# A graph attention kernel: queries stored once in DRAM, and stacked queries and keys loaded by two DMAs of 64 partitions each

## The chip, the cores and the metric

The kernel runs on one core of one Trainium2 chip. The metric is the device time of one execution in microseconds (us), lower is better. The core has five engines with instruction streams of their own: TensorE (PE in the profile, with PEld for its weight loads), VectorE (DVE), ScalarE (ACT), GpSimd (POOL) and SyncE (SP, which here only issues DMAs). The transfers of SP, ACT and POOL are carried by the same 16 DMA engines.

## What is computed

Two layers work on 16 graphs of 1024 nodes with 256 features, in float32.

```python
# layer 0: masked attention with 8 heads of 32 features
h = relu(layernorm(x))
Q, K, V = h @ Wq.T + bq, h @ Wk.T + bk, h @ Wv.T + bv
scores = Q @ K.T * 32 ** -0.5                  # per graph and head, 1024 x 1024
attn = softmax(where(adj == 0, -inf, scores))
x = x + (attn @ V) @ Wo.T + bo
# layer 1: attention whose scores depend on the kind of edge
h = relu(layernorm(x))
e_k = leaky_relu((h * a_k) @ h.T, 0.2)         # k = 0..3
alpha = softmax(e_{adj-1} where adj in 1..4, else -9e15)
x = x + alpha @ h
```

`adj` holds 0 and 1 here, so layer 1 needs only `e_0`. The kernel checks that at run time and has a general path, which the profiled execution does not take.

## The kernel before, in words

A **tile** is 128 nodes (rows) of one graph. There are 8 tiles in a graph and 128 in all, and the main loop `for s in range(B * NT + 1)` does the attention of one tile per pass. Inside a pass, a loop over the 8 heads writes out by hand (`tc.manual_schedule()`) what each engine does, in order. Besides the attention of tile `s` (`now`) a pass holds the rest of the tile before (`was`), layer 1 of the tile that is nine behind (`edge`), and the preparation of a tile of the next graph (`piece`, `piece_was`: normalise, transpose, project to Q, K and V).

**Scores with split numbers.** TensorE multiplies in the format float32r. To keep precision, Q and K are each held as two halves, a rounded number and the remainder. A head has 32 features, so the two halves of Q times the two halves of K are 4 x 32 = 128 rows of contraction, just the 128 partitions: `Attend.scores` (L455) multiplies `qt[:, h, :]` (128 partitions by 128 queries) with `keysets[b][h]` (128 partitions by 1024 keys), in two matmuls of 512 columns. In `qt` each feature's two halves must stand twice, and so must they in the keys, so that every half of Q meets every half of K.

**How the stacks are made.** The projections give features on partitions. The halves are written to DRAM and read back in the stacked order:

- Keys: `write_keys` (L325) writes both halves to `kds[b]`, laid out `[NC, P, 2, N]`. `load_key` (L355) reads the 64 rows of a head (32 features by 2 halves), each twice, by one DMA of 128 partitions, 512 KB, on SP's queue.
- Queries: `write_queries` (L319) writes the halves to `qds[b]` *twice*, by two DMAs (one per block of 128 features) of 256 KB on POOL's queue, into `[NT, NC, P, 2, 2, P]`. For the first graph `split` does the same on the queues of SP and ACT (L292), four 512 KB DMAs on each. `load_queries` (L422) then reads a tile's stack, 128 partitions by 8 heads by 512 bytes, by one DMA on SP's queue.

**When the stacks are loaded.** `qt` has two buffers; the next tile's is loaded in the middle of a pass (at head 3), half a pass before its use. A head's keys have a single buffer (`k0` to `k7`) that holds a whole graph's keys for 8 passes, so the keys of the next graph can be loaded only as the last pass of a graph (`t == NT - 1`) is done with them. `KEY_STEPS = (6, 9, 10, 13, 16, 20, 22, 24)` sets the places in half-heads: keys 0 to 3 in the last pass of a graph, keys 4 to 7 in the first pass of the next. This turn from graph to graph comes 15 times. Key `h` is first used at head `h` of the first pass.

**SP's queue** is served in order. In each pass it also carries 20 DMAs `pT<-blocks` (`placed`, L381): after VectorE has transposed 32x32 blocks of a tile's probabilities, four DMAs each take 32 partitions of `blocks`, 128 KB, and lay them out over 128 partitions of `pT`. Four of a pass's eight heads and the layer 1 tile go this way; the other heads are transposed on TensorE (L574). SP also writes `x1d` (L536) and `out` (L691).

Of the kernel before, what the change touches and what calls it, by code (L numbers as in the profile page):

```python
# [8 lines left out]
F32 = mybir.dt.float32  # L9
# [8 lines left out]
P = 128  # L18
HEADS = 8
HD = 32  # L20
# [22 lines left out]
def gnn_kernel(  # L43
# [18 lines left out]
    nc = tc.nc  # L62
    B, N, D = x.shape
    NT = N // P
    NC = D // P
# [15 lines left out]
    dram = ctx.enter_context(tc.tile_pool(name="dram", bufs=2, space=bass.MemoryType.DRAM))  # L81
# [64 lines left out]
    def norm_of(mv):  # L146

        g = nc.gpsimd
        n = mv.shape[1]

        def place(name, dtype=F32):
            if n <= 4:
                return small.tile([P, 4], dtype, tag=name, name=name)[:, :n]
            places.append(name)
            return many[:, len(places) * n - n : len(places) * n].bitcast(dtype)

        places = []
        if n > 4:
            many = work.tile([P, D], F32, tag="wide", name="many", bufs=1)

        ve = place("ve")
        g.tensor_scalar(ve, mv[:, :, 1], EPS, None, ALU.add)
        r = place("r")
        g.tensor_tensor(r, ve, less_half.to_broadcast([P, n]), ALU.pow)
        shift = place("shift")
        g.tensor_tensor(shift, mv[:, :, 0], r, ALU.mult)
        g.tensor_scalar(shift, shift, -1.0, None, ALU.mult)
        return r, shift
# [12 lines left out]
    qds, kds, vs, keysets, weights = {}, {}, {}, {}, {}  # L181

    class Piece:
# [66 lines left out]
        def project(self, which, oc):  # L250
            wT, bias = ((weights["wkT"], bk_t), (weights["wqT"], bq_t))[which]
            b, w = self.b, self.n * P
            if b not in kds:
                kds[b] = dram.tile([NC, P, 2, N], F32, tag="kd", name=f"kd_{b}")
            if b not in qds and which == 1:
                qds[b] = dram.tile([NT, NC, P, 2, 2, P], F32, tag="qd", name=f"qd_{b}")
            if self.n > 1:
                ps = ps_tr.tile([P, w], F32, tag="tr", name="proj")
            else:
                ps = (late, early)[which][:, oc * P : (oc + 1) * P]  # L260
            for fc in range(NC):
                nc.tensor.matmul(
                    ps,
                    lhsT=wT[:, fc, oc * P : (oc + 1) * P],
                    rhs=(self.hT, self.hTm)[which][:, fc, :],
                    start=(fc == 0),
                    stop=(fc == NC - 1),
                )

            self.projected.append((which, oc, ps, bias))  # L270
# [10 lines left out]
        def split(self):  # L281
            which, oc, ps, bias, halves, parts = self.halved.pop(0)
            nc.vector.scalar_tensor_tensor(
                parts[:, 1], ps, bias[:, oc : oc + 1], parts[:, 0].bitcast(F32), ALU.add, ALU.subtract
            )
            halves = halves.bitcast(F32)
            if which == 0:
                self.write_keys(oc, halves, nc.sync)
            elif self.n > 1:
                to = qds[self.b][self.first : self.first + self.n, oc]  # L290
                for twice in range(2):
                    (nc.sync, nc.scalar)[twice].dma_start(  # L292
                        out=to[:, :, twice].rearrange("t p w n -> p t (w n)"),
                        in_=halves.rearrange("p (t x) -> p t x", t=self.n),
                    )
            else:
                self.queries.append((oc, halves))

# [7 lines left out]
        def halve(self, which):  # L306
            halves = self.buffer(3, [P, NC, 2, P], F32R)
            nc.gpsimd.tensor_copy(halves[:, :, 0], self.full)
            nc.gpsimd.tensor_tensor(halves[:, :, 1], self.full, halves[:, :, 0].bitcast(F32), ALU.subtract)  # L309
            places = [(oc, halves[:, oc].bitcast(F32).rearrange("p w n -> p (w n)")) for oc in range(NC)]  # L310
            if which == 0:
                for oc, place in places:
                    self.write_keys(oc, place, nc.gpsimd)
            else:
                self.queries = places

        def write_queries(self):
            for oc, halves in self.queries:
                nc.gpsimd.dma_start(  # L319
                    out=qds[self.b][self.first, oc].rearrange("p u w n -> p u (w n)"),  # L320
                    in_=halves.unsqueeze(1).to_broadcast([P, 2, 2 * P]),
                )

        def write_keys(self, oc, halves, queue):
            queue.dma_start(  # L325
# [26 lines left out]
    def load_key(b, h):  # L352
        kt = keys.tile([P, N], F32R, tag=f"k{h}", name=f"k{h}_{b}")
        c, r = divmod(h, GROUP)
        nc.sync.dma_start(  # L355
            out=kt.bitcast(F32),
            in_=kds[b][c, r * HD : (r + 1) * HD]
            .rearrange("d w n -> (d w) n").unsqueeze(1).to_broadcast([2 * HD, 2, N]),
        )
        keysets.setdefault(b, {})[h] = kt  # L360


# [47 lines left out]
    class Attend:  # L410
# [7 lines left out]

        def load_queries(self):
            self.qt = work.tile([P, HEADS, P], F32R, tag="qt")  # L420
            q = qds[self.b][self.t].rearrange("c (r d) u w n -> (d u w) (c r) n", d=HD)
            nc.sync.dma_start(out=self.qt.bitcast(F32), in_=q)  # L422

        def load(self):
            self.adj = work.tile([P, N], I32, tag="adj", bufs=1)
# [344 lines left out]
    with tc.manual_schedule():  # L770
# [14 lines left out]
        r, shift = norm_of(mv)  # L785
# [8 lines left out]
        for which in range(2):  # L794
            for piece in first:
                for oc in range(NC):
                    piece.project(which, oc)
                    piece.high()
                    piece.split()
            if which == 0:  # L800
                for h in range(HEADS):
                    load_key(0, h)
# [16 lines left out]
        for s in range(B * NT + 1):  # L819
            b, t = divmod(s, NT)  # L820

            def load_keys(h, end):
                if t == NT - 1 and b + 1 < B and 2 * h + end in KEY_STEPS:
                    load_key(b + 1, KEY_STEPS.index(2 * h + end))
                if t == 0 and 0 < b < B and 2 * (HEADS + h) + end in KEY_STEPS:
                    load_key(b, KEY_STEPS.index(2 * (HEADS + h) + end))
# [216 lines left out]
```

## Time and profile before

| | |
|---|---|
| median of 3 runs | 3138.88 us (3132.21 to 3140.22) |
| the profiled execution | 3143.69 us, of which the span from its first to its last instruction is 3141.9 us |
| PE busy | 2941.3 us, 94% of the span, mean granted clock 0.984 |
| ACT, DVE, POOL busy | 2598.8, 2512.8, 2172.4 us |
| DMA traffic | 729.22 MB, mean 232 GB/s |
| `pT<-blocks` (SP) | 2560 DMAs of 128 KB, 3.6 us from issue to landing |
| `k<-kd` (SP) | 128 DMAs of 512 KB, 6.1 us |
| `qt<-qd` (SP) | 128 DMAs of 512 KB, 4.4 us |
| `qd<-halves` (POOL) | 240 DMAs of 256 KB, 3.0 us |

A row of the profile names the line of the kernel, the engine, the operation and the tiles (`out<-in`). In a timeline the columns are start, duration, engine, line, operation, count, and in brackets the idle time before and what ended it. A row of windows gives a stretch of the span, its length, each engine's busy time in it (with its number of instructions), the granted clock of TensorE as a share, the mean busy share of the 16 DMA engines, and the GB/s that they moved. The DMA share adds up packets by their starts, so in a short stretch it can pass 1.

### The profile page before, as it was taken

Reading aid. Unit: us, or ns where it says so; the run is one execution under the profiler, and the core shown is the slowest. Engines: PE = TensorE matmul, PEld = TensorE weight load, DVE = VectorE, ACT = ScalarE, POOL = GpSimd, SP = SyncE. Lnnn points to the kernel's source line nnn. Section 1 sums busy time; section 2 is a strip of 40 time slices with the busy share of each in tenths; the row PEclk is TensorE's granted clock in tenths of the full one; section 3 lists DMA queues with packets and bytes.
Section 4 is the critical chain, followed back from the end, with each engine's and each line's share of the span. In section 5 each row is a group of like instructions: output and inputs, shape, how many; then the busy total and the mean of one; then the engine's idle time right before and its main releaser. Section 6 shows DMA issues by size and latency. Waiting matters only on the chain. (4 is left out here: it accounts for less than half of the span.)

```text
span 3141.9 us, 95789 instructions
## 1 busy us (share of the span) xinstructions
PE 2941.3 (94%) x36210; PEld 2202.9 (70%) x36210; DVE 2512.8 (80%) x4391; ACT 2598.8 (83%) x5157; POOL 2172.4 (69%) x2995
## 2 busy tenths in 40 slices
PE   5888999899999999999999999999999999998987
PEld 3666777677676777777777676777767777676663
DVE  4777888788787887878888787888878788787874
ACT  3888989889888988889889898888978888787871
POOL 2666777777777776777777777777767777675542
PEclk8999999999999999999999999999999999999999
DMA  6676787877878787787877878787787877777663
GB/s 214 208 245 212 230 272 220 270 217 230 255 229 263 223 263 225 226 268 223 270 227 235 251 234 257 228 258 229 234 261 215 271 223 227 245 232 239 185 174 96
DMA packets 634692, 729.22 MB, mean 232 GB/s; under 512 B 67376, under 2 KB 565424, under 8 KB 634224
## 3 DMA queue, kind: packets, MB, share of 16 engines
q1 hardware_dynamic: 565152, 510.86, 54.5%
q0 software_dynamic: 66960, 210.04, 20.5%
q8 instruction: 291, 4.77, 0.6%
q10 hardware_dynamic: 2112, 2.10, 0.2%
q14 instruction: 177, 1.45, 0.1%
HBM read 252.98 MB, written 134.22 MB: 123 GB/s over the span
## 5 line engine op out<-in xcount | busy, mean ns | idle before, releaser
L467 DVE CUSTOM_DVE_ANT_0 p<-s,neg 128x1024 f32<-128x1024 f32 x1024 | 1235.6, 1207 | 274.5 <-PE s L455 241.3
L475 ACT ACTIVATE p<-p,nmx 128x1024 f32<-128x1024 f32 x1024 | 1182.2, 1155 | 205.0 <-DVE nmx L467 202.5
L455 PE MATMUL s<-k,qt 128*128 128x512 f32 x2048 | 764.9, 455 | 107.9 <-DMA k<-kd 72.5
L376 DVE STREAM_TRANSPOSE blocks<-p 128x1024 f32<-128x1024 f32 x520 | 643.7, 1238 | 20.5 <-ACT p L663 10.6
L575 ACT COPY pT<-trp 128x512 f32<-128x512 f32 x1024 | 547.0, 590 | 106.2 <-PE trp L574 106.2
L510 PE MATMUL acc<-pT,v 128*32 128x128 f32 x16384 | 559.0, 281 | 37.1 <-DMA pT<-blocks 22.1
L510 PEld LDWEIGHTS acc<-pT,v 128*32 128x32 f32 x16384 | 472.6, 113 | 156.5 <-issue 82.9
L574 PE MATMUL trp<-ident,p 128*128 128x128 f32 x4096 | 531.2, 273 | 1.6 <-ACT pT L575 1.5
L574 PEld LDWEIGHTS trp<-ident,p 128*128 128x128 f32 x4096 | 478.1, 140 | 73.2 <-ACT pT L575 3.1
L435 POOL TENSOR_SCALAR neg<-adj 128x1024 bf16<-128x1024 int32 x128 | 467.6, 3653 | 79.5 <-ACT neg L447 70.2
L681 PE MATMUL acc<-h,pT 128*32 128x256 f32 x8192 | 494.7, 383 | 8.8 <-DVE ot L690 8.8
L455 PEld LDWEIGHTS s<-k,qt 128*128 128x128 f32 x2048 | 324.3, 192 | 215.5 <-issue 79.5
L681 PEld LDWEIGHTS acc<-h,pT 128*32 128x32 f32 x8192 | 241.8, 110 | 211.9 <-issue 63.8
L659 POOL TENSOR_TENSOR sel<-sel,less 128x1024 f32<-128x1024 f32 x120 | 286.6, 2388 | 64.9 <-ACT less L648 44.9
L616 PE MATMUL s<-h1T,ha 128*128 128x512 f32 (+2 forms) x744 | 272.8, 490 | 2.6 <-ACT h1T L553 1.3
L657 POOL TENSOR_SCALAR less<-top 128x1 f32<-128x1 f32 x120 | 31.6, 264 | 274.5 <-DVE top L639 274.5
L319 POOL DMA_DIRECT2D qd<-halves x240 | 177.0, 777 | 58.7 <-POOL halves L309 31.8
L494 POOL COPY wide<-rec 128x256 f32<-128x256 f32 x128 | 53.9, 421 | 226.5 <-DVE rec L492 226.5
L475 ACT ACTIVATION_READ_ACCUMULATOR p<-p,nmx 128x1 f32 x1024 | 202.7, 198 | 0.0
L325 POOL DMA_DIRECT2D kd<-halves x240 | 171.7, 764 | 35.4 <-POOL halves L309 35.4
L309 POOL TENSOR_TENSOR halves<-full,halves 128x256 fp32r<-128x256 f32 x240 | 176.3, 735 | 20.6
L648 ACT ACTIVATE less<-sel 128x1024 f32<-128x1024 f32 x120 | 127.0, 1058 | 65.6 <-DVE top L639 65.6
(120 smaller groups left out, 4238.8 us busy)
## 6 DMA issues: line engine op xcount, KB each, us to landing
pT<-blocks SPq DMA_DIRECT2D x2560, 128.0 KB, 3.6
k<-kd SPq DMA_DIRECT2D x128, 512.0 KB, 6.1
qt<-qd SPq DMA_DIRECT2D x128, 512.0 KB, 4.4
adj<-in_adj POOLq DMA_DIRECT2D x127, 512.0 KB, 5.1
qd<-halves POOLq DMA_DIRECT2D x240, 256.0 KB, 3.0
kd<-halves POOLq DMA_DIRECT2D x240, 128.0 KB, 4.0
xb<-in_x POOLq DMA_DIRECT2D x128, 128.0 KB, 4.4
x1d<-x SPq DMA_DIRECT2D x128, 128.0 KB, 4.0
```

The lines of the kernel that those rows point to most:

```text
L319: nc.gpsimd.dma_start(out=qds[self.b][self.first, oc].rearrange("p u w n -> p u (w n)"), in_=halves.unsqueeze(1).to_broadcast([P, 2, 2 * P]),)
L376: nc.vector.transpose(blocks.rearrange("p b j q -> p j b q"), p)
L435: nc.gpsimd.tensor_scalar(self.neg, self.adj, 0.0, MASKED, ALU.is_equal, ALU.mult)
L455: nc.tensor.matmul(self.ps[:, cols], lhsT=self.qt[:, h, :], rhs=keysets[self.b][h][:, cols], start=True, stop=True,)
L467: nc.vector.tensor_tensor_reduce(out=p, in0=sides[h in (4, 6)], in1=self.neg, scale=-SCALE, scalar=FLOOR, op0=ALU.add, op1=ALU.min, accum_ ...
L475: nc.scalar.activation(p, p, AF.Exp, bias=nmx, scale=-1.0, accum_out=self.sums[:, h : h + 1])
L510: nc.tensor.matmul(sums_place[r * HD : (r + 1) * HD, g * P : (g + 1) * P], lhsT=vs[self.b][:, j, place_of(h) : place_of(h) + HD], rhs=self ...
L574: nc.tensor.transpose(tr[:, j, :], p[:, jj * P : (jj + 1) * P], ident)
L575: copy(pT[:, half * 4 : half * 4 + 4, :], tr)
L616: nc.tensor.matmul(self.side[:, cols], lhsT=self.ha[:, c, :], rhs=h1T[:, c, cols], start=(c == 0), stop=(c == NC - 1),)
L659: nc.gpsimd.tensor_tensor(self.sel, self.sel, self.less, ALU.subtract)
L681: nc.tensor.matmul(sums_place[a * HD : (a + 1) * HD, :], lhsT=self.pT[:, j, a], rhs=h1s[self.b][:, j, :], start=(j == 0), stop=(j == NT - 1),)
```

## The change

Queries are stored once: `qds[b]` loses the axis of copies, a tile's two blocks of 128 features go out by one POOL DMA instead of two (256 KB in all instead of 512 KB), and the first graph's queries are written by ACT's queue alone (SP's four DMAs go). The stacks are read by two DMAs of 64 partitions each. For `qt`, both DMAs read the same 64 rows (32 features by 2 halves), one to partitions 0 to 63 and one to 64 to 127. For the keys, the first takes the 32 rows of the rounded half, each twice, and the second the 32 rows of the remainder, each twice. The order of the 128 contraction rows changes in both operands alike.

```diff
@@ Piece.project
-                qds[b] = dram.tile([NT, NC, P, 2, 2, P], F32, tag="qd", name=f"qd_{b}")
+                qds[b] = dram.tile([NT, NC, P, 2 * P], F32, tag="qd", name=f"qd_{b}")
@@ Piece.split
                 to = qds[self.b][self.first : self.first + self.n, oc]
-                for twice in range(2):
-                    (nc.sync, nc.scalar)[twice].dma_start(
-                        out=to[:, :, twice].rearrange("t p w n -> p t (w n)"),
-                        in_=halves.rearrange("p (t x) -> p t x", t=self.n),
-                    )
+                nc.scalar.dma_start(
+                    out=to.rearrange("t p x -> p t x"), in_=halves.rearrange("p (t x) -> p t x", t=self.n)
+                )
@@ Piece.halve
-                self.queries = places
+                self.queries = halves.bitcast(F32).rearrange("p c w n -> p c (w n)")
@@ Piece.write_queries
-            for oc, halves in self.queries:
-                nc.gpsimd.dma_start(
-                    out=qds[self.b][self.first, oc].rearrange("p u w n -> p u (w n)"),
-                    in_=halves.unsqueeze(1).to_broadcast([P, 2, 2 * P]),
-                )
+            nc.gpsimd.dma_start(
+                out=qds[self.b][self.first].rearrange("c p x -> p c x"), in_=self.queries
+            )
@@ load_key
-        nc.sync.dma_start(
-            out=kt.bitcast(F32),
-            in_=kds[b][c, r * HD : (r + 1) * HD]
-            .rearrange("d w n -> (d w) n").unsqueeze(1).to_broadcast([2 * HD, 2, N]),
-        )
+        for w in range(2):
+            nc.sync.dma_start(
+                out=kt[w * 2 * HD : (w + 1) * 2 * HD].bitcast(F32),
+                in_=kds[b][c, r * HD : (r + 1) * HD, w].unsqueeze(1).to_broadcast([HD, 2, N]),
+            )
@@ Attend.load_queries
-            q = qds[self.b][self.t].rearrange("c (r d) u w n -> (d u w) (c r) n", d=HD)
-            nc.sync.dma_start(out=self.qt.bitcast(F32), in_=q)
+            q = qds[self.b][self.t].rearrange("c (r d) (u n) -> (d u) (c r) n", d=HD, u=2)
+            for w in range(2):
+                nc.sync.dma_start(out=self.qt[w * 2 * HD : (w + 1) * 2 * HD].bitcast(F32), in_=q)
```

## The prediction

> **What bounds the kernel now.** I read the page's engine line, then windows of single passes, the tensor engine's waits, and the timelines of PE and SP around one turn from graph to graph.
>
> ```profile
> PE 2941.3 (94%) x36210; PEld 2202.9 (70%) x36210; DVE 2512.8 (80%) x4391; ACT 2598.8 (83%) x5157; POOL 2172.4 (69%) x2995
> 1543.80:1571.30 27.50, 23.60 (x290) 18.17 (x286) 19.63 (x35) 20.04 (x40) 18.05 (x28) 0.94 0.94 311
> ...
> 1618.10:1640.80 22.70, 22.70 (x289) 17.31 (x285) 19.39 (x35) 20.65 (x42) 17.48 (x24) 1.00 0.75 228
> ```
>
> The last row is an ordinary pass (the fourth of a graph): 22.70 us, all of them PE's, with the DMA engines busy 0.75 of the time. The row above is the first pass of a graph: 27.50 us, PE 23.60, clock 0.94, DMA share 0.94. Summed over the 15 turns, the first passes take 441.30 us with PE busy 350.26, so 6.1 us idle each; the fourth passes take 340.80 us with 339.27. So ordinary passes are PE's alone; only the 15 turns, and the start, have time to win or lose to a DMA.
>
> ```profile
> PE s L455 <- DMA k<-kd: 72.5, 36, 5.8
> PE acc L510 <- DMA pT<-blocks: 22.1, 25, 2.2
> ...
> PE s L455 <- DMA qt<-qd: 15.5, 3, 14.7
> ```
>
> Those are PE's waits for DMAs (total, times, longest): keys first. Of the wait for `qt`, 14.7 us are one wait, at the start. One turn, PE and then SP:
>
> ```profile
> 1552.26 0.70 PE L455 MATMUL s<-k,qt 128*128 128x512 f32 x2 [1.30 <-DMA k<-kd]
> ...
> 1568.74 0.70 PE L455 MATMUL s<-k,qt 128*128 128x512 f32 x2 [1.21 <-DMA k<-kd]
> ```
>
> ```profile
> 1532.49 0.55 SPq L355 DMA_DIRECT2D k<-kd  x1
> 1533.87 2.54 SPq L381 DMA_DIRECT2D pT<-blocks  x4
> 1536.52 0.54 SPq L422 DMA_DIRECT2D qt<-qd  x1
> 1537.15 1.90 SPq L355 DMA_DIRECT2D k<-kd  x2
> ...
> 1545.67 0.93 SPq L355 DMA_DIRECT2D k<-kd  x1
> 1546.71 3.76 SPq L381 DMA_DIRECT2D pT<-blocks  x4
> ...
> 1562.65 0.54 SPq L422 DMA_DIRECT2D qt<-qd  x1
> 1563.24 0.72 SPq L355 DMA_DIRECT2D k<-kd  x1
> ```
>
> PE waits for key 3 (issued 1545.67, used 1552.26) and key 7 (1563.24, 1568.74). Both took 5.5 to 6.6 us to use, where a quiet 512 KB load (`qt<-qd`) lands in 4.4. What they wait in is the DMA queue:
>
> ```profile
> 1537.20:1552.10 14.90, 13.66 (x175) 10.53 (x166) 13.34 (x23) 13.18 (x27) 11.42 (x20) 1.00 1.01 333
> 1552.10:1568.60 16.50, 13.98 (x166) 9.96 (x166) 10.39 (x21) 12.05 (x24) 10.26 (x11) 0.90 0.90 300
> ...
> 1530.00:1533.00 3.00, 3.00 (x70) 2.55 (x69) 2.64 (x7) 2.57 (x5) 1.89 (x3) 1.00 0.77 214
> 38.00:47.00 9.00, 7.58 (x66) 7.15 (x64) 3.49 (x9) 3.00 (x7) 5.68 (x6) 1.00 1.04 410
> ```
>
> The last two numbers of a row are DMA share and GB/s. From key 1's issue to key 3's use the engines are full (1.01); until key 7's use, 0.90.
>
> **The change part by part.**
>
> *q's second copy.* 240 POOL DMAs become 120; each removed one takes 777 ns of POOL (L319's group), 93 us in all. POOL waits 274.5 us for VectorE's `top` (L639) alone and nearly nothing waits for POOL on these lines, so 0; if it did gate a pass, 0.8 us each. In DMA time a pass loses 256 KB: 262144 B at 410 GB/s (38 to 47 us, a full queue of 128-partition transfers) is 0.64 us. In an ordinary pass that is hidden, PE being full; in a turn one such write (1539.8) stands ahead of key 3.
>
> *More issues.* One more per `qt`, at 0.54 us: 128 x 0.54 = 69 us of SP; one more per key, at 0.61: 78 us. An ordinary pass has about 15 us of SP issues in 22.7, and `qt` is issued half a pass early: 0. In a turn, key 3's second half goes out 0.6 us later and key 7's 0.54 + 0.6 = 1.1 later, `qt` being just ahead. But with a full queue, both halves wait behind others' bytes anyway: 0 in the main case.
>
> *A second landing to wait for.* Scores now wait for two DMAs. A bare wait (PEldq EVENT_SEMAPHORE) takes 51 ns; 128 for `qt` and 128 for keys make at most 13 us. In ordinary passes weight loads run ahead of a full PE: 0, and 13 for the range.
>
> *The 64-partition loads: the disputed cost.* No DMA of before writes part of the partitions. The nearest row is 1530 to 1533, where only `pT<-blocks` runs, each reading 32 partitions: 214 GB/s, at a DMA share of 0.77. The full-queue row gives 410/1.04 = 394 GB/s per fully busy engines, this one 214/0.77 = 278. So something slows such packets by 1.42. A key (524288 B) at 410 takes 1.28 us; at 1.42 times that, 1.81 (+0.53); at 214 GB/s as it stands, 2.45 (+1.17). Issue alone caps that row near 131072 B per 0.65 us = 202 GB/s, so it doesn't prove 214 to be the ceiling. Ends: 0 (reading is not writing) and +1.17 per key. I take +1.17, since in that row the four DMAs of a group touch different quarters and so may help one another, while key halves come as two on end. For `qt`, whose 512-byte pieces are slower by themselves, I take half, +0.6.
>
> The Trainium skill has a rule against this change ("SBUF — State Buffer", Door 1: The DMA port swizzle): partitions 0 to 63 reach only 8 of 16 DMA ports, and it measures 196 GB/s for 64 partitions against 328 for 128 at 1 MiB; two DMAs, one on each half, gain 6%. By its ceilings, 218 and 436 GB/s, a key would cost 1.2 us more, an estimate that gives about the sum below; by the row's milder reading it is a quarter of that.
>
> *Sum per turn, at +1.17.* Up to key 3: keys 1, 2, 3 stand in a full queue, 3 x 1.17 = 3.5, `qt` +0.6, q's copy -0.64: +3.5 us on PE. (Key 0 lands 6.9 us ahead of use: 0.) Then keys 4 to 7, 4 x 1.17 = 4.7, and `qt` +0.6, less idle DMA time 0.10 x 16.5 = 1.65, less half of the 3.5 us in which PE's stop lets the queue drain: +1.9. Together 5.4. A stop also lowers the clock: first passes have PE busy 23.35 us against 22.62 in fourth ones, 0.73 for 6.1 idle, so 12% on top: 6.1. Fifteen turns: +91.
>
> *The start.*
>
> ```profile
> 31.20 10.15 SPq L355 DMA_DIRECT2D k<-kd  x8
> 46.00 7.19 SPq L292 DMA_DIRECT2D qd<-p  x4
> 56.96 0.36 SPq L422 DMA_DIRECT2D qt<-qd  x1
> ```
>
> The first scores wait until 61.0. SP's four writes go, so `qt` can be issued around 46 instead of 57, but queues behind the eight keys: 4 MB at 410 GB/s is 10.2 us, at 214 it is 19.6. Ends: 8 us earlier (keys at full rate, done by about 51 as now), 2 later. I take 4 earlier.
>
> Sum: +91 - 4 = +87. Span 3141.9 + 87 = 3228.9; the profiled execution has 1.8 us around its span and lies 4.8 above the median, so 3225.9. I predict **3226 us**.
>
> **Rivals.**
>
> *The queue gets shorter (faster).* If 64 partitions load at full rate, only the bytes saved count: key 3 lands 0.64 us earlier, x 1.12 x 15 = -11, and the start -8: 3120. For it: `pT<-blocks` reads, keys write, and 333 GB/s flow in the turn with such DMAs in the mix. Against: the 0.77 share at 214 GB/s.
>
> *SP's issues or a mild price decide (a little slower).* Full-rate loads, but the later second halves count: key 3 +0.6, key 7 +1.1, x 1.12 x 15 = +29, start -8: +21, 3160. At +0.53 per key: up to key 3 1.6 + 0.3 - 0.64 = 1.3, after it 2.1 + 0.3 - 1.65 - 0.6 = 0.2; 1.5 x 1.12 x 15 = +25, start -4: +21, 3160 again. For it: in 1546.71 four issues take 3.76 us instead of 2.5, so SP is short of room too. It decides if a key pair lands within 0.6 us of what one did.
>
> *Nothing measurable*: small price and savings cancel, 3139.
>
> *All of it lands on PE*: no idle DMA time and no draining helps, `qt` +1.17: 4.0 + 5.9 = 9.9 x 1.12 x 15 = +166, start +2: 3307.
>
> **How the numbers follow.** Forecast, with prices toward the full one, 0.55 (3180 to 3290); up to 0.04 of it beyond. SP or mild price 0.23 (3150 to 3180). Faster 0.14. Nothing 0.08. The range 3135 to 3290 leaves out the faster case and the far end. A run can tell about 0.3%, 9 us, from no change: faster 0.14, within 0.08, slower 0.78.
>
> **What would show it.** Right: PE's wait for `k<-kd` at L455 grows from 72.5 to about 150 us; first passes go from 29.4 to about 35 us while fourth passes stay at 22.7; the second key DMA lands over 6.5 us after its issue; GB/s in 1537 to 1552's counterpart drops below 333 at a share still near 1. The start's wait for `qt` shrinks by 4. Wrong: first passes at 29 us or less; key waits unchanged; or ordinary passes longer, which would mean that `qt` or the second waits reach PE. What I can't see in this trace is a write to half the partitions.

## The result, and the profile after

The changed kernel takes 3241.11 us (median of 4 runs, 3231.47 to 3252.96); the kernel before, run beside it, takes 3139.55 (4 runs). The ratio is 1.0324, with a 95% interval of 1.0279 to 1.0368: **slower by 3.2%**. The profiled execution took 3243.49 us, with a span of 3241.6, 99.7 us more than that of before.

From the page of the changed kernel: the engine line, one line of the DMA queues (packets, MB, and the time of the packets as a share of 16 engines' span), and two of the DMA issues (KB each, median us to landing):

```profile
PE 2983.2 (92%) x36210; PEld 2230.1 (69%) x36210; DVE 2513.2 (78%) x4391; ACT 2597.6 (80%) x5157; POOL 2089.5 (64%) x2875
q1 hardware_dynamic: 567136, 508.78, 56.1%
k<-kd SPq DMA_DIRECT2D x256, 256.0 KB, 5.9
qt<-qd SPq DMA_DIRECT2D x256, 256.0 KB, 4.1
```

POOL has 120 instructions and 83 us less, as counted, and nothing came of it. PE is busy 42 us longer with the same 36210 matmuls. Where the time lies is seen in the windows of the changed kernel, for the same graph as before: the first pass, the fourth, and the two halves of the turn (from key 1's issue to key 3's use, and from there to key 7's):

```profile
1601.10:1637.70 36.60, 27.10 (x290) 20.05 (x286) 20.29 (x35) 20.95 (x41) 20.14 (x29) 0.86 0.97 269
1684.70:1707.40 22.70, 22.70 (x288) 17.28 (x284) 19.35 (x35) 20.52 (x42) 16.54 (x24) 1.00 0.73 214
...
1596.00:1612.60 16.60, 12.35 (x159) 9.96 (x151) 12.51 (x20) 11.96 (x25) 9.61 (x19) 1.00 1.04 290
1612.60:1632.50 19.90, 15.67 (x166) 10.32 (x166) 9.85 (x19) 12.19 (x24) 13.04 (x18) 0.83 0.97 242
```

The fourth pass is the one of before to the hundredth: 22.70 us, all PE's. The first pass went from 27.50 to 36.60 us; of the 9.1 us, 3.5 are PE itself at a clock of 0.86, and 5.6 are idle. This turn is one of the dearer ones. The sums and means over all 15 first passes, before and in the changed kernel:

```profile
sum 441.30, PE 350.26 PEld 267.68 DVE 294.12 ACT 300.65 POOL 293.49; mean PE 23.35 PEld 17.85 DVE 19.61 ACT 20.04 POOL 19.57
sum 524.70, PE 380.73 PEld 284.44 DVE 295.62 ACT 303.48 POOL 286.27; mean PE 25.38 PEld 18.96 DVE 19.71 ACT 20.23 POOL 19.08
```

So a mean first pass is some 5.6 us longer: 2.0 us of PE's busy time, for the same matmuls, and 3.5 us in which PE is idle. PE's waits in the changed kernel (total, times, longest):

```profile
PE s L452 <- DMA k<-kd: 126.1, 50, 8.1
PE s L452 <- DMA qt<-qd: 28.1, 4, 15.0
PE acc L507 <- DMA pT<-blocks: 19.6, 21, 2.1
```

The keys make 72.5 into 126.1, and `qt` 15.5 into 28.1: a new wait. PE's timeline shows both. The first three rows are of the turn, where keys 3, 6 and 7 now stop PE; the last is in the first graph's third pass, where `qt` did not:

```profile
1613.62 1.05 PE L452 MATMUL s<-k,qt 128*128 128x512 f32 x2 [5.15 <-DMA k<-kd]
1627.29 0.70 PE L452 MATMUL s<-k,qt 128*128 128x512 f32 x2 [0.78 <-DMA k<-kd]
1633.52 0.70 PE L452 MATMUL s<-k,qt 128*128 128x512 f32 x2 [2.58 <-DMA k<-kd]
...
106.37 1.19 PE L452 MATMUL s<-k,qt 128*128 128x512 f32 x2 [4.02 <-DMA qt<-qd]
```

Last, SP's queue in the changed kernel, at the start and in the same turn (start, us, count):

```profile
31.41 19.72 SPq L352 DMA_DIRECT2D k<-kd  x16
51.23 1.27 SPq L419 DMA_DIRECT2D qt<-qd  x2
...
1603.54 2.75 SPq L352 DMA_DIRECT2D k<-kd  x2
1606.51 3.56 SPq L377 DMA_DIRECT2D pT<-blocks  x4
...
1620.97 1.24 SPq L352 DMA_DIRECT2D k<-kd  x2
1622.38 2.54 SPq L377 DMA_DIRECT2D pT<-blocks  x4
1624.96 1.40 SPq L419 DMA_DIRECT2D qt<-qd  x2
1626.41 1.28 SPq L352 DMA_DIRECT2D k<-kd  x2
```

In the last four rows, start and duration together give the next row's start within 0.2 us: SP does nothing but issue here, and every added DMA pushes those behind it. The two rows of key 3 and of the blocks behind it hold waits as well: two issues take 2.75 us there, and 1.24 at 1620.97. The second half of key 3 goes out at 1605.76, 0.02 us after the second half of key 2, eight DMAs ahead of it in the queue, has landed.

Cut at the first score matmul of each pass, the two traces give this account (what follows the last tile's first scores, +0.7, is left out):

| stretch | change, us | predicted |
|---|---|---|
| start, to the first scores (61.04 to 61.59) | +0.6 | -4 |
| the first graph's passes | +20.5 | 0 |
| the 15 turns (first passes 29.42 to 34.96 in the mean) | +83.2 | +91 |
| all other passes | -5.2 | 0 |

### The profile page after: what moved, and what is told of

Its sections match the earlier page's. It is cut to its first block, busy times and chain, and to the rows that moved or that the text cites. A ratio compares the mean times of both kernels' runs of the same rounds, so it can differ in the third digit from the quotient of the medians.

```text
span 3241.6 us, 96087 instructions
## 1 busy us (share of the span) xinstructions
PE 2983.2 (92%) x36210; PEld 2230.1 (69%) x36210; DVE 2513.2 (78%) x4391; ACT 2597.6 (80%) x5157; POOL 2089.5 (64%) x2875
## 5 line engine op out<-in xcount | busy, mean ns | idle before, releaser
L452 PE MATMUL s<-k,qt 128*128 128x512 f32 x2048 | 776.3, 461 | 171.5 <-DMA k<-kd 126.1
L507 PE MATMUL acc<-pT,v 128*32 128x128 f32 x16384 | 575.9, 287 | 33.5 <-DMA pT<-blocks 19.6
L507 PEld LDWEIGHTS acc<-pT,v 128*32 128x32 f32 x16384 | 484.7, 115 | 157.7 <-ACT recT L501 62.3
L571 PE MATMUL trp<-ident,p 128*128 128x128 f32 x4096 | 538.7, 275 | 1.6 <-ACT pT L572 1.5
L571 PEld LDWEIGHTS trp<-ident,p 128*128 128x128 f32 x4096 | 485.9, 142 | 76.3 <-issue 4.1
L613 PEld LDWEIGHTS s<-h1T,ha 128*128 128x128 f32 x744 | 126.7, 190 | 70.7 <-issue 45.2
```

Source lines behind the costliest of these rows:

```text
L452: nc.tensor.matmul(self.ps[:, cols], lhsT=self.qt[:, h, :], rhs=keysets[self.b][h][:, cols], start=True, stop=True,)
L507: nc.tensor.matmul(sums_place[r * HD : (r + 1) * HD, g * P : (g + 1) * P], lhsT=vs[self.b][:, j, place_of(h) : place_of(h) + HD], rhs=self ...
L571: nc.tensor.transpose(tr[:, j, :], p[:, jj * P : (jj + 1) * P], ident)
L613: nc.tensor.matmul(self.side[:, cols], lhsT=self.ha[:, c, :], rhs=h1T[:, c, cols], start=(c == 0), stop=(c == NC - 1),)
```

## The experiments

The theories were: **half rate** (a DMA to 64 partitions moves its bytes more slowly, the forecast's main price); **number** (each load as two DMAs costs, whatever partitions they write: by the 0.6 us that SP takes to issue one, or by the place among the DMAs in flight that one holds); and **bytes** (the saved second copy of q). All runs are timed against the kernel before on the same chip. The stretches come from one profiled execution each, so a few us in them mean nothing.

| kernel | median | ratio, 95% | start | first graph | turns (mean first pass) | others |
|---|---|---|---|---|---|---|
| the change | 3241.11 | 1.0324 (1.0279 to 1.0368) | +0.6 | +20.5 | +83.2 (34.96) | -5.2 |
| `e1_keys_halves` | 3198.66 | 1.0190 (1.0163 to 1.0216) | +5.5 | +0.7 | +57.4 (33.24) | -1.9 |
| `e4_keys_columns` | 3188.27 | 1.0172 (1.0132 to 1.0213) | -0.4 | -0.3 | +42.3 (32.24) | +0.1 |
| `e2_queries_halves` | 3178.37 | 1.0140 (1.0103 to 1.0177) | +0.9 | +11.6 | +23.1 (30.95) | -1.0 |
| `e7_stride_two` | 3216.42 | 1.0251 (1.0221 to 1.0281) | -3.7 | +16.3 | +71.8 (34.21) | -9.1 |
| `e5_queries_heads` | 3161.20 | 1.0060 (1.0041 to 1.0079) | +0.1 | -1.6 | +19.5 (30.72) | +1.6 |
| `e8_idle_issues` | 3227.05 | 1.0283 (1.0255 to 1.0310) | +2.0 | -0.3 | +86.0 (35.15) | -0.7 |
| `e9_keys_by_pool` | 3169.68 | 1.0088 (1.0072 to 1.0104) | +0.7 | -2.2 | +31.2 (31.50) | -3.7 |
| `e10_once_one_load` | 3113.74 | 0.9914 (0.9892 to 0.9936) | -5.9 | -1.6 | -15.5 (28.39) | -10.1 |
| `e11_keys_456_by_pool` | 3180.94 | 1.0110 (1.0096 to 1.0125) | -0.3 | -2.8 | +54.3 (33.04) | -6.1 |
| `e12_and_nodes_by_pool` | 3176.44 | 1.0098 (1.0083 to 1.0114) | +0.1 | -3.0 | +56.2 (33.17) | -10.3 |
| `e13_halves_adj_later` | 3200.80 | 1.0181 (1.0161 to 1.0201) | +0.5 | +0.6 | +22.1 (30.89) | +35.9 |
| `e14_fewer_blocks_in_turn` | 3112.75 | 0.9920 (0.9899 to 0.9940) | 0.0 | -0.4 | -36.4 (26.99) | +3.1 |

### One part alone: the keys, by partitions and by columns

Both leave q as before and read each key by two DMAs of 256 KB. The first gives each DMA 64 neighbouring partitions:

```diff
+        for i in range(2):
+            rows = kds[b][c, r * HD + i * (HD // 2) : r * HD + (i + 1) * (HD // 2)]
+            nc.sync.dma_start(out=kt[i * 2 * HD : (i + 1) * 2 * HD].bitcast(F32),
+                in_=rows.rearrange("d w n -> (d w) n").unsqueeze(1).to_broadcast([HD, 2, N]))
```

> The kernel before with one part of the change: each head's keys come by two DMAs of 64 neighbouring partitions (the first 16 features, then the last 16); queries as before. Theory H (a DMA that writes 64 neighbouring partitions moves its bytes at about half the rate): the turns lose what they lost in the whole change or a little more, as q's second copy is still written: first passes 35 to 36 us against 29.4, the first graph's seven passes unchanged, +85 to +100 us, 3215 to 3245. Theory N (it is the number of DMAs: one more issue and landing per key): the same sign, but the same loss must come from any other cut of a key into two DMAs. Theory Q (the loss sits with the queries' loads): within 10 us of before.

The second gives each DMA half the columns, on all 128 partitions:

```diff
+        rows = kds[b][c, r * HD : (r + 1) * HD].rearrange("d w n -> (d w) n")
+        for i in range(2):
+            cols = slice(i * HALF, (i + 1) * HALF)
+            nc.sync.dma_start(out=kt[:, cols].bitcast(F32),
+                in_=rows[:, cols].unsqueeze(1).to_broadcast([2 * HD, 2, HALF]))
```

> The kernel before with each head's keys cut into two DMAs of 512 columns, each over all 128 partitions: the same bytes and the same number of DMAs as two halves, with 2 KB pieces. Theory H: within 15 us of before (3125 to 3155), first passes 29 to 30.5 us. Theory N: as slow as the two halves of 64 partitions, first passes 35 us, 3215 or more.

The halves take 3198.66 us and the columns 3188.27. Their intervals overlap, so for the keys alone the totals do not separate the theories; but the columns, with all partitions in every DMA, already bring +42.3 us to the turns, and the partitions only 15.1 on top. The landings and the queue's packets do separate, first by partitions, then by columns:

```profile
q1 hardware_dynamic: 567200, 510.87, 56.2%
k<-kd SPq DMA_DIRECT2D x256, 256.0 KB, 6.2
...
q1 hardware_dynamic: 583584, 510.87, 54.2%
k<-kd SPq DMA_DIRECT2D x256, 256.0 KB, 4.8
```

At the same 256 KB a DMA lands in 6.2 us (median) with 64 neighbouring partitions and in 4.8 with 128. Half rate is real, and it is the smaller part. The columns understate the price of the number, though: the first score matmul of a head reads the first 512 columns alone, and in the mean of the turns key 7's starts 27.3 us after the pass began, 1.2 us before its second DMA has landed (28.5).

### One part alone: the queries, by partitions and by heads

```diff
+            for i in range(2):
+                rows = slice(i * 2 * HD, (i + 1) * 2 * HD)
+                nc.sync.dma_start(out=self.qt[rows].bitcast(F32), in_=q[rows])
```

> The kernel before with one part of the change: a tile's stacked queries come by two DMAs of 64 neighbouring partitions; keys and the writes of q as before. Theory H with a load that has no slack in the first graph: passes 1 to 7 of the first graph grow by 3 to 4 us each (+20 to +27 us), first passes of later graphs by 0.5 to 1 us (+8 to +15), ordinary passes by nothing: 3165 to 3180. If queries are always early enough, as the prediction had it: first graph unchanged, +0 to +15, 3140 to 3155.

```diff
+            q = qds[self.b][self.t].rearrange("c (r d) u w n -> c (d u w) r n", d=HD)
+            for i in range(NC):
+                heads = slice(i * GROUP, (i + 1) * GROUP)
+                nc.sync.dma_start(out=self.qt[:, heads].bitcast(F32), in_=q[i])
```

> The kernel before with a tile's stacked queries cut into two DMAs of four heads each, both over all 128 partitions (same bytes, same 512-byte pieces, one DMA more). Of two halves of 64 partitions the first graph's passes lost 11.6 us and the turns 23.1. Theory N (the added DMA itself costs: an issue of 0.65 us in SP's queue and one of the eight places for DMAs in flight): nearly the same here, first graph +8 to +12, turns +15 to +23, 3160 to 3180. Theory H (the half rate of 64 neighbouring partitions): under +10 us in all, 3135 to 3150.

In the turns the two are alike: +23.1 and +19.5 us. They differ in the first graph: +11.6 with the halves, -1.6 with the heads, where head 0 needs only the first DMA and the second has until head 4. (This cut, too, understates the price of a second DMA that the first scores wait for.) The first graph's loss is thus the landing of a *second* half that the first scores need.

### The same change with every second partition

`e7_stride_two` is the changed kernel in bytes, DMAs and issues, but each DMA writes every second partition over all 128:

```diff
-                out=kt[w * 2 * HD : (w + 1) * 2 * HD].bitcast(F32),
+                out=kt[w::2].bitcast(F32),
-                nc.sync.dma_start(out=self.qt[w * 2 * HD : (w + 1) * 2 * HD].bitcast(F32), in_=q)
+                nc.sync.dma_start(out=self.qt[w::2].bitcast(F32), in_=q)
```

> The changed kernel with its two DMAs per stack writing every second partition instead of the lower and the upper 64: same DMAs, same bytes, same rows of DRAM, 64 partitions each. Theory H: the loss goes, since each DMA now spreads over all 128 partitions' places: 3120 to 3150, first passes 28.5 to 30 us, key waits of PE near 70 us, and the first graph's passes near those of before. Theory N: it stays at 3220 to 3250. A result between says how the two share the loss.

From its page, the queue line and the landing of the keys; then its windows' row for the same first pass:

```profile
q1 hardware_dynamic: 567136, 508.78, 53.5%
k<-kd SPq DMA_DIRECT2D x256, 256.0 KB, 4.8
```

```profile
1583.50:1619.70 36.20, 26.16 (x290) 18.73 (x286) 20.39 (x35) 21.04 (x41) 20.18 (x29) 0.86 0.83 274
```

These three lines settle most of it. With the same packets and bytes on queue q1, the changed kernel's packets took 0.561 x 3241.6 = 1818.5 us of 16 engines and these 0.535 x 3216.2 = 1720.7: neighbouring partitions cost 98 us of DMA time, and here it is gone. Yet the pass still takes 36.20 us, with the DMA engines now at 0.83 instead of 0.97 (0.86 and 0.97 in the mean of the 15 first passes), and PE waits for keys 120.6 us in all, against 126.1. So over a turn as a whole the engines have room, and the keys are late all the same. They are full only in parts of it: 0.97 from key 1's issue to just before key 3's use (1579.0 to 1592.9), and 0.92 while key 7 is in flight (1606.5 to 1614.8). Key 3 is used 9.4 us into the pass in the mean, where it was 9.2 in before and 11.5 in the change; what remains is mostly key 7, which SP issues later. In the total, half rate is worth 3241.11 - 3216.42 = 24.7 us, of which 11.4 lie in the turns.

SP's queue in this kernel, in the same turn:

```profile
1600.67 1.25 SPq L352 DMA_DIRECT2D k<-kd  x2
1602.09 2.50 SPq L377 DMA_DIRECT2D pT<-blocks  x4
1604.63 1.82 SPq L419 DMA_DIRECT2D qt<-qd  x2
1606.49 1.31 SPq L352 DMA_DIRECT2D k<-kd  x2
```

These rows have no gap over 0.2 us either. In the mean over the 15 turns, the second half of key 7 is issued 22.6 us after the pass began, where before's only DMA went out at 19.9, and it has landed at 29.6 instead of 26.2: 2.7 of the 3.4 us are the issue.

### The number of DMAs alone

`e8_idle_issues` is the kernel before with an idle DMA of 512 bytes, into a tile that nobody reads, behind each key load and each query load:

```diff
+        idle = small.tile([P, 1], F32, tag="idle", name="idle")
+        nc.sync.dma_start(out=idle, in_=bk.rearrange("(c p o) -> c p o", p=P, o=1)[0])
```

> The kernel before with a DMA of 512 bytes (128 pieces of 4) added on SP's queue behind every key load and every load of queries; nobody waits for its data. It adds issues and hardly any bytes. Theory N1 (SP's issue time in a turn): each costs 0.4 to 0.65 us of SP, eight or nine of them in a turn stand in a queue without gaps; key 7 about 2 us later, first passes +2 to +3 us, +30 to +50 us in all, 3170 to 3190. Theory N2 (the places in flight, each held for some 6 us): little, since these land fast: under +15 us. Theory H: nothing.

Its waits of PE, its line of DMA issues, and SP's timeline in the turn:

```profile
PE s L459 <- DMA k<-kd: 126.6, 49, 6.4
```

```profile
idle<-in_L_gnn_bk SPq DMA_DIRECT2D x256, 0.5 KB, 4.4
```

```profile
1598.62 0.54 SPq L355 DMA_DIRECT2D k<-kd  x1
1599.20 0.59 SPq L361 DMA_DIRECT2D idle<-in_L_gnn_bk  x1
1600.09 2.49 SPq L383 DMA_DIRECT2D pT<-blocks  x4
```

With full-width loads and hardly a byte more, the turns grow by 86.0 us, as much as in the change (83.2), and PE's wait for keys is the change's 126.1 to half a microsecond. The result lies above all three expectations. A turn holds some nine of them (one per key, one per `qt`, 0.59 us of SP each): 86.0 / 15 = 5.7 us per turn, 0.64 us each. That this is near one issue is partly chance, for 2.1 of the 5.7 us are slower matmuls and 3.65 are PE's idle time: key 7 goes out 3.4 us later than in before and lands 4.5 later. Their packets are not quite free, either: queue q1 took 0.544 x 3228.3 = 1756.2 us of 16 engines, where before took 0.545 x 3141.9 = 1712.3, so 44 us for 256 of them, 0.17 each. **The number of DMAs alone is enough for what the turns lost.** With the saved bytes of the next section and the half rate of the section before, the parts add up: 86.0 - 15.5 + 11.4 = +81.9 us, beside +83.2 measured.

How one costs, by SP's 0.59 us or by the place that it holds until it has landed (4.4 us), the traces tell in part. In none of those of the next table does SP start a DMA before its own DMA eight ahead has landed, while some start before the one seven ahead has (238 in before, 401 in the change). So a break of SP's that ends within 0.06 us of the landing of the DMA eight ahead (SP's and ACT's counted together) is a wait for a place. From key 1's issue to the end of key 7's, mean of the 15 turns, in us:

| kernel | DMAs of SP | length | SP's instructions | waits for a place | other waits |
|---|---|---|---|---|---|
| before | 29.7 | 27.1 | 20.4 | 1.8 | 3.5 (for VectorE) |
| the change | 37.7 | 30.9 | 24.1 | 4.6 | 0.4 |
| `e7_stride_two` | 37.7 | 28.5 | 24.7 | 1.4 | 0.3 |
| `e8_idle_issues` | 36.7 | 29.1 | 24.0 | 3.0 | 0.3 |

(Breaks under 0.1 us, 1.4 to 2.0 us in all, make up the rest.) Seven or eight more DMAs take 3.5 to 4.3 us more of SP's own time in all three, and use up the 3.5 us in which before's queue waited for VectorE's tiles. The places add 2.9 us in the change and 1.2 here, but nothing in `e7_stride_two`, whose turns lose 71.8 us all the same. So SP's time is the common part; the places come on top where landings are slow, as with 64 neighbouring partitions.

### The bytes alone

`e10_once_one_load` is the changed kernel with its single write of q, but one load of 128 partitions for each `qt` and each key. Its `qt` holds overlapping rows of the short layout, and so not the right queries:

```diff
+            rows = qds[self.b][self.t].rearrange("c p x -> (c p x)")
+            q = bass.AP(tensor=rows.tensor, offset=rows.offset, ap=[[P, P], [54 * P, HEADS], [1, P]])
+            nc.sync.dma_start(out=self.qt.bitcast(F32), in_=q)
```

> The changed kernel's single write of q alone: written once as there, but read by one DMA over 128 partitions and 8 heads of 512-byte pieces, with rows that overlap within the tile's 512 rows instead of standing twice (so the queries are not the right ones and the output is not the reference's; bytes, pieces and DMAs are those of one load); keys as before. It shows what the saved bytes are worth: 31 MB less to write. By the prediction's terms: start -4 to -8 us, turns -0.6 us each: -10 to -20 us, 3118 to 3132. If the bytes are worth nothing: 3130 to 3148.

3113.74 us: the shorter writes alone gain 0.9%, 5.9 us at the start, 15.5 in the turns, some 10 in the other passes. (Those 10 are not shown to come from the bytes: `e12_and_nodes_by_pool`, which writes q twice, has -10.3 there too.) So the change held a gain, and its loads cost the 102 us of the result and these 25 besides.

### Where else the keys can be issued

```diff
# e9
-        nc.sync.dma_start(
+        (nc.gpsimd if b else nc.sync).dma_start(
# e11, all keys but 4, 5 and 6 staying with SP
+        (nc.gpsimd if b and h in (4, 5, 6) else nc.sync).dma_start(
# e12: e11, and the write of x1d
-            nc.sync.dma_start(out=x1ds[self.b][self.rows, :], in_=self.x1)
+            nc.gpsimd.dma_start(out=x1ds[self.b][self.rows, :], in_=self.x1)
```

> The kernel before with the key loads of all graphs but the first issued by POOL instead of SP, as one DMA of 128 partitions each; nothing else is moved. Theory N: SP loses five issues in a first pass and three in the pass ahead of it, and five of its eight places in flight; keys 3 and 7 can go out earlier, first passes fall from 29.4 to 26 to 28 us, -20 to -50 us, 3090 to 3120. If only the bytes in the DMA queue count: within 10 us of before. If POOL holds the keys back behind its own waits (it waits 274 us in all for VectorE's top): slower, 3150 or more.

> The kernel before with only keys 4, 5 and 6 of all graphs but the first issued by POOL; keys 0 to 3 and 7 stay with SP, since POOL issued keys 1 and 7 late when it had them all. Theory N (DMAs in SP's queue are the price of a turn, 5.7 us for the nine idle ones, so about 0.6 each): three fewer in a first pass bring key 7 some 2 us earlier: first passes 27 to 28.5 us, -15 to -35 us, 3105 to 3125. If the bytes in the DMA queue bound the turn: within 8 us of before.

> As the run with keys 4, 5 and 6 by POOL, and the write of each tile's x1 to DRAM (L536) is issued by POOL too, one issue less on SP in each pass, just ahead of key 3 in a turn. Theory N: a further 0.6 us per turn, -5 to -15 us more than that run, 3095 to 3118. If POOL's own order makes something late: slower than that run.

None was faster, and of the theories only the last one for the first of these runs came out. With all keys on POOL, PE no longer waits for keys 4 to 6 at all, but POOL issues key 1 late, 1.4 us before the pass (SP does so 6.4 before), and PE waits for it in all 15 turns, 58.3 us; key 7 goes out at 23.0. With three keys on POOL, key 4 is issued 1.3 us into the pass, ahead of key 3 (2.4), and is there 9.7 us before its use. But key 3, with its use at 11.0, lands at 10.9, where it landed at 9.1 in before, and PE's waits for it are 58.5 us instead of 32.2. PE's waits for keys and for blocks in that kernel:

```profile
PE s L455 <- DMA k<-kd: 84.7, 30, 5.9
PE acc L510 <- DMA pT<-blocks: 41.7, 23, 3.2
```

For the blocks 22.1 became 41.7, and key 7, still SP's, went out at 24.2 instead of 19.9. The write of x1 on POOL changes nothing beyond the intervals. What is issued earlier delays what stands beside it: these runs were misses, and they show that up to key 3, where the DMA engines are full (a share of 0.99 from 6 us before the pass to key 3's use, in the mean of the turns, in before as here), the bytes ahead of a load count too, and not SP's issues alone.

### Why the first graph lost

`e13_halves_adj_later` is `e2_queries_halves` with the load of the adjacency, 512 KB by POOL, moved from head 4 to head 7.

```diff
-                    if nxt2:        # at head 4
-                        nxt2.load()
+                    if nxt2:        # at head 7
+                        nxt2.load()
```

> The kernel with the queries' load in two halves of 64 partitions (one part of the change), and the load of the tile after next's adjacency (512 KB on POOL's queue, issued just behind the queries' loads) put off from head 4 to head 7. If that load is what comes between the two halves of the queries in the first graph: the first graph's passes go back to within 4 us of before (+11.6 with the halves alone), the wait for qt falls to the one at the start; 3160 to 3175 in all, as the turns keep their +20. If the second half is late by itself: first graph still +8 to +14.

The first graph's +11.6 us is gone (+0.6), so the adjacency's load, which came between the two halves of `qt`, made the second one late. The traces show it too: in `e2_queries_halves`, for the third pass, the adjacency is issued at 98.85 and lands at 106.69, and the second half of `qt`, issued at 98.41, lands at 107.48, 5.5 us after the first; with the later adjacency the second lands 1.9 us after the first. The total is a miss all the same, 3200.80 us: the other passes lose 35.9, and PE's wait for `pT<-blocks` grows from 17.0 us in `e2_queries_halves` to 38.3. Why is not shown; only 1.0 us of waiting is put down to the adjacency itself.

### The other way round: fewer DMAs in a turn

If the number of DMAs in a turn costs, taking some away should gain. `e14_fewer_blocks_in_turn` is the kernel before, in which the first pass of graphs 1 to 15 transposes the probabilities of heads 0 and 1 on TensorE. That takes away 8 DMAs of 128 KB of `pT<-blocks` per turn.

```diff
+            if self.t == 0 and self.b and h < 2:
+                to = work.tile([P, N], F32, tag="p", name="p", bufs=4)
+                self.probs[h] = (to, nmx)
+                place = to.rearrange("p (c k b) -> p c b k", b=NB, k=HD)
+                p = p.rearrange("p (c b k) -> p c b k", b=NB, k=HD)
...
-                if turning and th in BY_BLOCKS:
+                if turning and th in BY_BLOCKS and not (turning.t == 0 and turning.b and th < 2):
```

> The kernel before, but in the first pass of every graph but the first, the probabilities of heads 0 and 1 are transposed on TensorE (with the exponential writing them in the order of the blocks) instead of by VectorE and SP's eight DMAs of 128 KB. A turn loses eight DMAs and 1 MB in SP's queue, and gains 16 transposes (about 2 us of PE) and four copies on ACT (2.4 us). Theory N, with bytes: the nine idle DMAs cost 5.7 us per turn, and keys moved ahead of the blocks only made the blocks late, so issues and bytes together bound a turn; taking eight away brings key 7 some 5 us earlier, and PE's idle 6 us shrink to 2 or 3: first passes 25.5 to 27.5 us, -25 to -55 us, 3085 to 3118. If something else holds keys 3 and 7 (the release of their buffers, VectorE): first passes 29 to 31 us, 3135 to 3165.

Its waits of PE:

```profile
PE acc L516 <- DMA pT<-blocks: 17.2, 25, 2.0
PE s L455 <- DMA k<-kd: 14.6, 14, 3.2
```

3112.75 us, 0.8% faster than the kernel before and 4.0% faster than the changed one. The wait for keys falls from 72.5 to 14.6 us, though PE does 240 matmuls more. Key 7 now goes out 12.6 us into the pass instead of 19.9, and PE never waits for it (32.6 us before). Key 3 lands no earlier, at 9.1; there the added transposes fill part of PE's wait. The run takes issues and bytes away together, and two block transposes of 1.24 us (mean) from VectorE, for which SP's queue waited 3.5 us in a turn of before. So it shows that key 7 is held by what stands ahead of it in SP's queue, not which of these counts.

## Why the prediction held, and where its steps did not

The forecast of 3226 us (3135 to 3290) holds, and so does its place: the turns, with first passes at 34.96 us ("about 35") and fourth passes at 22.7. Two of its signs came too: 290 GB/s at a share of 1.04 in the first half of the turn where 333 were, and key waits of 126.1 us (150 were expected). Two did not: a key's second DMA lands 6.1 us after its issue (median), not over 6.5, and the start's wait for `qt` did not shrink by 4 but went from 14.7 to 15.0. **And the sum is right by luck: errors in its terms cancel.** Half rate, which was to make nearly all of the loss, makes 11.4 us of the turns' 83.2; the number of DMAs, put at 0, makes 86.0 when it is added alone.

*"I take +1.17" per key: twice too much.* Of the two readings that I had, 1.17 us from the `pT<-blocks` row as it stands and 0.53 from its slower packets, the milder was the right one. Queue q1 took 0.562 x 3203.9 = 1800.6 us with halves by partitions and 0.542 x 3185.3 = 1726.4 by columns; 74.2 / 128 = 0.58 us of DMA time per key. Both kinds together took 98 us, which leaves (98 - 74) / 128 = 0.19 for a `qt`, where I took 0.6. The reason given for the dearer end, that quarters on end help one another and halves don't, was an argument with no row behind it. The Trainium skill ("SBUF — State Buffer", "Can I just issue two DMAs to hit both halves?") has the direction right: it asks for one transfer that spans all 128 partitions, and where each DMA spans them, in `e7_stride_two`, keys land in 4.8 us instead of 5.9. By the ceilings of the same page (Door 1: The DMA port swizzle) a key would be 1.2 us dearer, an estimate; the packets of this mixed traffic show 0.58, and the measurement decides.

*That price on the path: a further step too much.* I let most of the delayed bytes in a full queue land on PE, +91 us. Measured, half rate is worth 11.4 us in the turns (the change against `e7_stride_two`), or 15.1 for the keys alone. It does cost up to key 3, which PE uses 11.5 us into the pass instead of 9.4 in `e7_stride_two`. But most of that is no loss, since key 7 comes late from SP's queue in both: PE's waits for it are 51.2 us in the change and 72.6 in `e7_stride_two`.

*"With a full queue, both halves wait behind others' bytes anyway: 0 in the main case": the step that failed.* I counted only the issue just ahead of key 3 and the two ahead of key 7, and gave even these to a rival at +29 us. But delays add up along a queue with little room. In before, SP goes from key 3's issue to the end of key 6's, 1545.67 to 1558.20, with no break over 0.3 us, and a turn has 3.5 us of waits for VectorE to spare, which eight issues of 0.6 us use up; the rows were there to be read. In the change key 7's first half goes out 24.0 us after the pass begins instead of 19.9, and its second at 24.8, and 31.2 instead of 26.2 is when it lands. Keys 3 and 7 stop PE in all 15 turns, for 58.1 and 51.2 us where it was 32.2 and 32.6, and key 6 in 11 turns where it did in one. Idle DMAs alone make +86.0. The Trainium skill ("DMA: Bandwidth & Descriptors", Issuing engines are not separate DMA queues) calls the time that a sequencer takes to start a DMA usually small beside the DMA; these turns are a stretch where it can't be left out. The two prices also do not exclude each other, as my rival put it ("SP's issues or a mild price"): the mild price, the issues at their real size and the saved bytes were to be added.

*"12% on top" for the clock: too little.* PE's busy time in a mean first pass grew by 2.0 us for 3.5 us more of idle time, which is 57%, not 12. The forecast of 6.1 us per turn was 5.4 of idle and 0.7 of slower matmuls; measured are 3.5 and 2.0. I had read the share from before's own 6.1 us of idle, and it does not hold for the next 3.5. That is the second error that made the sum come out.

*q's second copy: undersized.* I took 0.64 us per turn and, at the start, 4: in all some 15. `e10_once_one_load` gives 25: 5.9 at the start, 15.5 in the turns, and some 10 in the other passes that may not be the bytes'.

*"`qt` is issued half a pass early: 0": wrong in the first graph.* The slack was read in an ordinary pass. In the first graph, `qt` for the third pass was issued at 96.74 and landed at 101.4 for a use at 101.7. In the change it goes out at 97.30, its halves land at 101.7 and 106.2, and PE waits 4.02 us. Seven passes make +20.5; `e13_halves_adj_later` shows the adjacency's load between the halves as the cause; here it is issued at 98.05 and lands at 105.37, 0.9 us ahead of the second half. POOL's 93 us were worth 0, as said: POOL became 83 us less busy, and no wait for it is among PE's first ones.

*The start, -4: it was +0.6.* SP no longer writes q, and `qt` goes out at 51.2 instead of 57.0, but behind 16 key DMAs that take 19.72 us to issue where 8 took 10.15, partly waiting for landings of ACT's writes of q. Spread over all partitions the start gains 3.7, and with single loads 5.9.

**What stays open.** How much of an added DMA's price is SP's 0.6 us and how much the place that it holds: no run adds the one without the other. For the places: SP's own waits for a key's landing grow from 4.7 + 8.9 = 13.6 us to 23.8 + 17.0 = 40.8 in the change, and SP's key loads also wait 6.3 us for ACT's writes of q. For the issues: in `e7_stride_two` a turn has no more waits for a place than in before. Keys by columns, queries by heads and the saved bytes make only +42.3 + 19.5 - 15.5 = +46.3 us in the turns, and `e7_stride_two` has +71.8; those two cuts let the first matmul start on the first DMA, and with the idle DMAs in their place the sum is 86.0 - 15.5 = +70.5. A single 128-partition load of the right rows from the short layout wasn't tried.

## What to carry to other kernels

Look for the stretches in which an issuing queue has few gaps, and add up what room it has: here 3.5 us in a turn. Beyond it each added DMA costs its 0.6 us of the queue, whatever its size, and the delays add up to the last load behind it. Count slower matmuls with a stop of PE: here 2.0 us with 3.5 of idle time. Splitting a load in two to save bytes elsewhere has to pay for that, and a split by partitions pays more than one that leaves every DMA all of them. Read a load's slack in every phase of the program, the first graph and the turns among them, not in an ordinary pass alone.

## What the runs showed of the hardware that was not expected

- Some nine DMAs of 512 bytes in a turn cost as much as the whole change: 5.7 us, 2.1 of them slower matmuls. One takes 0.59 us of SP and 4.4 us to land, about as long as 256 KB do (4.8).
- Two DMAs of 256 KB that each write 64 neighbouring partitions land in 5.9 us (median), those that write every second partition in 4.8, with the same packets. By partitions instead of columns, 512 KB of a key take 0.58 us more of DMA time, on the 1.28 estimated at 410 GB/s: far from twice as long.
- In these kernels SP starts no DMA before its own DMA eight ahead has landed (in none of the over 3000 of a trace), and its key loads at the start wait for the landing of DMAs that ACT issued (6.3 us in 3 waits): the two queues share what limits the DMAs in flight. Whether the chip or the program sets that limit is not shown.
- Behind a longer stop of PE its granted clock was lower: 1.00 up to key 3 and 0.83 from there to key 7 in this turn, where before it was 1.00 and 0.90. So 5.6 us more of idle time came with 3.5 us of slower matmuls.
